# Second attention of a transformer block: longest query tiles first, fill spread by share, fewer product pieces in the last group

## The chip, the cores and the metric

The kernel runs on one NeuronCore of a Trainium2 chip. Its engines work in parallel from queues of their own: TensorE (PE) multiplies matrices into PSUM, with its weight loads shown separately (PEld); VectorE (DVE), ScalarE (ACT) and GpSimd (POOL) work elementwise and reduce; SyncE (SP) starts DMA transfers. They wait for one another through semaphores. The metric is the device time of one execution in microseconds (us), as a median over runs; a profile of one more execution shows where its time goes.

## The reference

A block of four steps over x of 1024 tokens and 512 channels, each `x = x + step(layernorm(x))`: a first attention of 32 heads, an expert layer, a second attention, and the expert layer again. The change touches the second attention alone. It has 32 query heads of width 128 in 8 groups; the 4 heads of a group share keys and values:

```
q = (x @ Wq.T).reshape(b, s, H, HD).transpose(0, 2, 1, 3)
k, v = likewise with Wk, Wv and HKV = 8 heads
q, k = rmsnorm(q) * q_norm_w, rmsnorm(k) * k_norm_w
scores = einsum('bkgqd,bksd->bkgqs', qg, k) / sqrt(HD)
bias = where(rel > 0, NEG_INF, slopes * rel)
attn = softmax(scores + bias, axis=-1)
out = einsum('bkgqs,bksd->bkgqd', attn, v) ... @ Wo.T
```

It is causal: query tile i (128 tokens, i = 0 to 7) sees the first (i + 1) x 128 keys, so tile 7 has eight times the columns of tile 0. All arithmetic is float32.

## The kernel before, in words

The second attention (`attention_b`) loops over groups g, heads hh and query tiles i. For one tile, `softmax(g, hh, i)` makes the scores on TensorE in pieces of up to 512 keys (L778; two PSUM buffers), adds the bias on VectorE (L780), takes the row maximum (L784, scaled at L785), exponentiates on ScalarE with the row sum beside it (L787), takes the reciprocal on VectorE (L789) and normalises on GpSimd (L790). The result p is transposed in 32 x 32 blocks on VectorE by `columns`: the first five key tiles into one buffer PT (L805), which each head overwrites, the last three into TT (L811), which has a place for each head of a group.

`product(g, hh, i0, i1)` multiplies the transposed weights of query tiles i0 to i1, and of the first five key tiles, with the values. It uses matmuls of 32 rows, four of them side by side (L822, tile `o`; one PSUM buffer of four banks), in the order of the key tiles; ScalarE copies the result to oT (L847). `product_rest(g, heads)` does the same with the last three key tiles, for one or more heads at once (L822, tile `or`), and VectorE adds it to oT (L863). In the program one such float32 matmul shows as two instructions.

Between tiles TensorE gets other work, the *fill*: for the next group the projections of keys and values (L687, 8 units of four matmuls) and of queries (L732, 32 units of one matmul, evicted at L741 on ScalarE and L742 on VectorE once in four; sums of squares at L758 and L762), and for the group before the output projection (L628, 32 units, its addition to x on VectorE at L633 once in four units). Their PSUM tiles come from a pool of two buffers. After each tile the loop takes units from the fill until a count `due` is reached: before, `units * n // 32` after n of a group's 32 tiles, with units = 74 (42 in group 0). The last group has no next one; its own counts are in the code: the rest of group 6's output projection in heads 0 and 1, nothing until the 20th tile, and then its own output projection of heads 0 and 1 (two units and one addition for each token tile) and of head 2. Its weights are loaded when head 2 begins. The output projection of head 3 runs in the expert layer that follows.

`finish` of a tile is called two tiles later (LAG = 2): it transposes p, and at the end of a head calls `product`, at the end of a group the rest of all four heads. The last group is different: each head is multiplied in two halves (tiles 0 to 3, then 4 to 7), followed by its own rest. When the program is built, the order of the instructions on each engine may be altered where the dependencies permit.

Of the kernel before, what the change touches and what calls it, by code (L numbers as in the profile page):

```python
# [18 lines left out]
NT = T // P  # L19
# [16 lines left out]
HKV = 8  # L36
GRP = HB // HKV
# [27 lines left out]
class Block:  # L65
# [546 lines left out]
    def attention_b(self, ctx, wo_pool, WqT, WkT, WvT, WoT, qw, kw, xnT, missing, ffn_weights):  # L612
# [9 lines left out]
        oTs = {}  # L622

        def project_o(g, wo, heads, ps_m, tag):
            for t in range(NT):
                ps = ps_m.tile([P, C], F32, tag=tag, name=f"wo{g}_{heads[0]}_{t}")
                for h in heads:
                    nc.tensor.matmul(  # L628
                        ps, lhsT=oTs[g, h][:, t * P : (t + 1) * P], rhs=wo[:, h, :], start=(h == heads[0]), stop=(h == heads[-1])
                    )  # L630
                    if h < heads[-1]:
                        yield
                nc.vector.tensor_add(self.x[t], self.x[t], ps)  # L633
                yield

        with ExitStack() as ctx:
# [23 lines left out]
            def load_qkv(g):  # L660
                wkv = wp.tile([P, self.FFN_SMALL], F32, tag="wkv", name=f"wkv{g}")
                wkv = wkv[:, : KC * 2 * DB].rearrange("p (k n d) -> p k n d", k=KC, n=2)
                for n, src in enumerate((WkT, WvT)):
                    nc.sync.dma_start(wkv[:, :, n, :], src[:, g * DB : (g + 1) * DB].rearrange("(k p) n -> p k n", p=P))
                wq = wp.tile([P, KC, GRP * DB], F32, tag="wq", name=f"wq{g}")
                nc.sync.dma_start(wq, WqT[:, g * GRP * DB : (g + 1) * GRP * DB].rearrange("(k p) n -> p k n", p=P))
                return wq, wkv

            def load_o(g):
                wo = wo_pool.tile([P, GRP, C], F32, tag="wo", name=f"wo{g}")  # L670
                nc.sync.dma_start(wo, WoT[g * GRP * DB : (g + 1) * GRP * DB, :].rearrange("(h p) n -> p h n", p=P))
                return wo
# [130 lines left out]
            def columns(hh, p, i):  # L803
                m = min(JS, i + 1)
                nc.vector.transpose(  # L805
                    PT[:, i : i + (NT - 1) * (m - 1) + 1 : NT - 1, :], p[:, : m * P].rearrange("p (j k) -> p j k", k=P)
                )
                m = i + 1 - JS
                if m > 0:
                    at = i - JS  # L810
                    nc.vector.transpose(  # L811
                        TT[:, hh, at : at + (JT - 1) * (m - 1) + 1 : JT - 1, :],
                        p[:, JS * P : (JS + m) * P].rearrange("p (j k) -> p j k", k=P),
                    )

            def by_groups(g, o, cols, js, moving):

                for j in js:
                    for b in range(NB):
                        for a in range(NB):  # L820
                            rows = slice(a * B, (a + 1) * B)
                            nc.tensor.matmul(  # L822
                                cols(o[:, a], j),
                                lhsT=vs[g][rows, j * NB + b, :],
                                rhs=moving(j, rows, slice(b * B, (b + 1) * B)),
                                start=(j == js[0] and b == 0),
                                stop=(j == js[-1] and b == NB - 1),
                            )

            def queries(t, i0, i1):  # L830

                return t[:, i0 * P : i1 * P].rearrange("p (i a c) -> p a i c", a=NB, c=B)

            def product(g, hh, i0, i1):

                n = i1 - i0
                o = ps_o.tile([P, NB, QC], F32, tag="o", name=f"o{g}_{hh}_{i0}")
                by_groups(
                    g,
                    o,  # L840
                    lambda o, j: o[:, max(j - i0, 0) * B : n * B],
                    range(min(JS, i1)),
                    lambda j, rows, ks: PT[rows, (NT - 1) * j + max(j, i0) : (NT - 1) * j + i1, ks],
                )
                if i0 == 0:
                    oTs[g, hh] = otp.tile([P, T], F32, tag="oT", name=f"oT{g}_{hh}")
                nc.scalar.copy(queries(oTs[g, hh], i0, i1), o[:, :, : n * B].rearrange("p a (i c) -> p a i c", c=B))  # L847

            def product_rest(g, heads):

                n, h0 = len(heads), heads[0]
                o = ps_o.tile([P, NB, QC], F32, tag="o", name=f"or{g}_{h0}")
                by_groups(
                    g,
                    o,
                    lambda o, j: o[:, : n * JT * B].rearrange("p (h q) -> p h q", h=n)[:, :, (j - JS) * B :],
                    range(JS, NT),
                    lambda j, rows, ks: TT[rows, h0 : h0 + n, (JT - 1) * (j - JS) + j - JS : (JT - 1) * (j - JS) + JT, ks],
                )
                for h in heads:  # L860
                    to = queries(oTs[g, h], JS, NT)
                    more = o[:, :, (h - h0) * JT * B : (h - h0 + 1) * JT * B].rearrange("p a (i c) -> p a i c", c=B)
                    nc.vector.tensor_add(to, to, more)  # L863

            def in_turn(*gens):
                for g in gens:
                    yield from g
# [8 lines left out]
            heads = list(range(GRP))  # L876
            rest = []

            def finish(g, hh, i, p):
                while rest:  # L880
                    product_rest(*rest.pop(0))
                columns(hh, p, i)
                if g == HKV - 1:

                    if i == NT // 2 - 1:
                        product(g, hh, 0, NT // 2)
                    elif i == NT - 1:
                        product(g, hh, NT // 2, NT)
                        product_rest(g, [hh])
                elif i == NT - 1:  # L890
                    product(g, hh, 0, NT)
                    if hh == GRP - 1:
                        rest.append((g, heads))

            for g in range(HKV):


                last = g == HKV - 1
                parts = []
                if not last:  # L900
                    wq, wkv = load_qkv(g + 1)
                    parts.append(project_kv(g + 1, wkv))
                    parts.append(project_q(g + 1, wq))
                if g:
                    parts.insert(-1, project_o(g - 1, wo, heads, ps_m, "m"))
                fill = in_turn(*parts)
                units = 74 if g else 42
                done = 0
                for hh in range(GRP):
                    if g and hh == 2:  # L910
                        if last:
                            for _ in fill:
                                pass
                        wo = load_o(g)
                        if last:
                            fill = in_turn(project_o(g, wo, [0, 1], ps_m, "m"), project_o(g, wo, [2], ps_m, "m"))
                    for i in range(NT):
                        p = softmax(g, hh, i)
                        n = hh * NT + i + 1
                        if not last:  # L920
                            due = units * n // (GRP * NT)
                        elif hh < 2:
                            due = max(0, (n - 2) * 32 // 14)
                        else:
                            due = 32 + max(0, 2 * (n - 19)) if n < 27 else 48 + (n - 27)
                        while done < due:
                            next(fill, None)
                            done += 1
                        pending.append((g, hh, i, p))
                        if len(pending) > LAG:  # L930
                            finish(*pending.pop(0))
                    if last and hh == GRP - 1:
                        for item in pending:
                            next(fill, None)
                            finish(*item)
                for _ in fill:
                    pass
                if g == HKV - 2:

                    self.load_ffn(wp, nc.sync, ("wkv", "wq"), *ffn_weights)  # L940
# [156 lines left out]
```

## Time and profile before

| | us |
|---|---|
| runs: median (lowest to highest of 3) | 1710.32 (1709.41 to 1710.95) |
| the profiled execution's own time | 1710.8 |
| its span, first to last instruction | 1709.0 |
| TensorE matmul busy | 1663.4 (97%) |
| VectorE busy | 1110.7 (65%) |
| ScalarE busy | 540.0 (32%) |
| GpSimd busy | 348.8 (20%) |
| second attention, from its first scores | 569 to 1649 |
| expert layer after it | 1649 to 1709 |

How to read the views: a *window* row gives the busy time of each engine within a stretch, and how many instructions it had (x); PEclk is the granted clock of TensorE, 1.00 being full speed. A *group* row gives line, engine, operation, tiles (out<-in), shapes and count, then busy time, the mean of one in ns, and the idle time before such instructions with what ended it. A *wait* row names who waited for whom: us in total, how often, and the longest. A *timeline* row gives start, duration and count of instructions of one kind in sequence; the end of a matmul is modelled and lies some tenths of a microsecond behind the start of the next row, so stretches are measured from start to start.

### The profile page before, as it was taken

How to read it: one execution, taken by the hardware profiler on the slowest of the kernel's cores; microseconds unless marked ns; L12 is line 12 of the kernel's file. 1: busy time of each engine (PE TensorE's matmuls, PEld its weight loads, DVE VectorE, ACT ScalarE, POOL GpSimd, SP SyncE). 2: the span in 40 equal slices, each digit the busy share in tenths (PEclk: the TensorE clock that was granted, in tenths of full speed). 3: DMA queues.
4: the chain of work that ended last, by engine and by line, in shares of the span. 5: the costliest groups of instructions: out<-in, count | busy, mean ns of one | idle time of the engine just before them, and what ended most of it. 6: DMA issues, size and time to landing. Idle time of an engine off the chain costs nothing.

```text
span 1709.0 us, 32010 instructions
## 1 busy us (share of the span) xinstructions
PE 1663.4 (97%) x13040; PEld 940.1 (55%) x13040; DVE 1110.7 (65%) x2872; ACT 540.0 (32%) x1201; POOL 348.8 (20%) x512
## 2 busy tenths in 40 slices
PE   5999999999998999999999999999999999999988
PEld 2544334333555566655665756655665566566654
DVE  3456666663462688677667676677667766777772
ACT  1315555556211333233223223223223322322220
POOL 3000000000311323113212222222311321222140
PEclk9999999999999999999999999999999999999998
DMA  5000000000003210200200110020020021000001
GB/s 191 1 1 2 1 2 1 2 1 1 1 1 112 71 29 26 62 26 26 61 28 1 55 41 19 29 59 26 26 63 26 25 59 37 1 26 26 2 1 49
DMA packets 60356, 51.92 MB, mean 30 GB/s; under 512 B 5489, under 2 KB 46961, under 8 KB 60209
## 3 DMA queue, kind: packets, MB, share of 16 engines
q1 hardware_dynamic: 57840, 43.83, 8.8%
q10 hardware_dynamic: 1584, 3.15, 0.5%
q0 software_dynamic: 784, 2.90, 0.5%
q8 instruction: 102, 1.67, 0.4%
q14 instruction: 46, 0.37, 0.1%
HBM read 30.98 MB, written 2.10 MB: 19 GB/s over the span
## 4 chain that ended last, share of the span: by engine, by line
PE 86%; DVE 10%; ACT 1%; POOL 1%; DMA 1%; issue 0%; SPq 0%; DVEq 0%; ACTq 0%; POOLq 0%
PE o L822 13%; PE pq L732 12%; PE s L778 12%; PE wo L628 9%; PE kv L687 7%; PE sT L347 7%; PE oT L378 4%; PE s L295 3%; PE pm_f L588 3%; PE or L822 3%; DVE p L780 3%; DVE nm L784 2%; DVE pT L805 2%; PE pj_q L166 2%; PE pj_v L166 2%; PE pm_ao L981 2%
## 5 line engine op out<-in xcount | busy, mean ns | idle before, releaser
L790 POOL TENSOR_SCALAR p<-p,rs 128x128 f32<-128x128 f32 (+7 forms) x256 | 190.2, 745 | 751.3 <-DVE rs L789 686.4
L787 ACT ACTIVATE p<-p,nm 128x128 f32<-128x128 f32 (+7 forms) x256 | 198.1, 774 | 453.5 <-DVE nm L785 443.2
L780 DVE SCALAR_TENSOR_TENSOR p<-s,rq,rel 128x512 f32<-128x512 f32 (+3 forms) x384 | 227.6, 607 | 119.5 <-PE s L778 118.9
L778 PE MATMUL s<-kT,qT 128*128 128x512 f32 (+3 forms) x768 | 294.8, 492 | 1.9 <-DVE p L780 1.5
L732 PE MATMUL pq<-xnTb,wq 128*128 128x512 f32 x512 | 246.2, 599 | 0.0
L628 PE MATMUL wo<-wo,oT 128*128 128x512 f32 x512 | 242.0, 594 | 3.4 <-DVE x L633 1.9
L778 PEld LDWEIGHTS s<-kT,qT 128*128 128x128 f32 x768 | 141.2, 190 | 165.9 <-issue 126.4
L822 PEld LDWEIGHTS o<-pT,va 32*128 32x128 f32 x5632 | 215.7, 185 | 28.3 <-DVE rs L789 11.8
L822 PE MATMUL o<-pT,va 32*128 32x128 f32 (+7 forms) x5632 | 224.7, 313 | 0.7
L805 DVE STREAM_TRANSPOSE pT<-p 128x640 f32<-128x640 f32 (+4 forms) x256 | 172.2, 674 | 72.8 <-PE o L822 54.5
L363 ACT ACTIVATE p<-sT 128x512 f32<-128x512 f32 (+1 forms) x320 | 157.5, 557 | 124.9 <-PE s L295 65.9
L784 DVE TENSOR_REDUCE nm<-p 128x1 f32<-128x128 f32 (+7 forms) x256 | 188.6, 737 | 3.6
L295 PE MATMUL s<-kT,qT 32*128 32x512 f32 (+3 forms) x768 | 178.3, 522 | 1.4 <-ACT p L363 1.4
L347 PE MATMUL sT<-qTm,kT 32*128 32x512 f32 (+3 forms) x768 | 152.5, 519 | 0.0
L628 PEld LDWEIGHTS wo<-wo,oT 128*128 128x128 f32 x512 | 93.8, 190 | 87.0 <-issue 72.0
L732 PEld LDWEIGHTS pq<-xnTb,wq 128*128 128x128 f32 x512 | 92.3, 190 | 87.9 <-issue 80.2
L687 PE MATMUL kv<-wkv,xnTb 128*128 128x256 f32 x512 | 118.4, 385 | 9.0 <-DVE nm L785 4.0
L687 PEld LDWEIGHTS kv<-wkv,xnTb 128*128 128x128 f32 x512 | 96.9, 192 | 31.5 <-DVE nm L785 6.9
L312 DVE TENSOR_REDUCE part<-s 128x1 f32<-128x512 f32 x128 | 80.8, 685 | 38.8 <-PE s L295 34.3
L347 PEld LDWEIGHTS sT<-qTm,kT 32*128 32x128 f32 x768 | 59.1, 183 | 66.2 <-issue 22.3
L403 POOL TENSOR_TENSOR o<-os,rsa 128x64 f32<-128x64 f32 x64 | 16.7, 292 | 369.0 <-DVE rsa L401 364.6
L847 ACT COPY oT<-o 128x1024 f32<-128x1024 f32 (+1 forms) x36 | 33.0, 917 | 181.6 <-PE o L822 176.4
(154 smaller groups left out, 1690.8 us busy)
## 6 DMA issues: line engine op xcount, KB each, us to landing
va<-v SPq DMA_DIRECT2D x256, 64.0 KB, 2.0
wq<-in_b_WqT_dram SPq DMA_DIRECT2D x8, 1024.0 KB, 5.3
wo<-in_b_WoT_dram SPq DMA_DIRECT2D x8, 1024.0 KB, 5.3
x<-in_x_dram SPq DMA_DIRECT2D x8, 256.0 KB, 7.9
wkv<-in_b_WkT_dram SPq DMA_DIRECT2D x8, 256.0 KB, 3.1
wkv<-in_b_WvT_dram SPq DMA_DIRECT2D x8, 256.0 KB, 3.4
out_dram<-x SPq DMA_DIRECT2D x8, 256.0 KB, 2.0
wq<-in_a_wqT_dram ACTq DMA_DIRECT2D x1, 1024.0 KB, 6.2
```

The source lines that it names most:

```text
L295: nc.tensor.matmul(made[j][:, at:end], lhsT=qT[rows_of(j), c, i * P : (i + 1) * P], rhs=kT[rows_of(j), c, kc * QC : kc * QC + end - at], s ...
L347: nc.tensor.matmul(made[j][:, at:end], lhsT=kT[rows_of(j), c, b * P : (b + 1) * P], rhs=qTm[c, qc][rows_of(j), QC - (end - at) :], start=n ...
L628: nc.tensor.matmul(ps, lhsT=oTs[g, h][:, t * P : (t + 1) * P], rhs=wo[:, h, :], start=(h == heads[0]), stop=(h == heads[-1]))
L687: nc.tensor.matmul(ps.rearrange("p a b -> p (a b)"), lhsT=xnT[:, kc, i * P : (i + 1) * P], rhs=wkv[:, kc].rearrange("p a b -> p (a b)"), s ...
L732: nc.tensor.matmul(ps, lhsT=wq[:, kc, hh * DB : (hh + 1) * DB], rhs=xnT[:, kc, cols], start=(kc == 0), stop=(kc == KC - 1))
L778: nc.tensor.matmul(s, lhsT=qT[:, i * P : (i + 1) * P], rhs=kT[:, lo:hi], start=True, stop=True)
L780: nc.vector.scalar_tensor_tensor(p[:, lo:hi], s, rq[:, i : i + 1], rel[:, at + lo : at + hi], ALU.mult, ALU.add)
L784: nc.vector.tensor_reduce(nm, p[:, :w], AX.X, ALU.max, negate=True)
L787: nc.scalar.activation(p[:, :w], p[:, :w], AF.Exp, bias=nm, scale=slope, accum_out=ss)
L790: nc.gpsimd.tensor_scalar(p[:, :w], p[:, :w], rs, 1.0, ALU.mult, ALU.mult)
L805: nc.vector.transpose(PT[:, i : i + (NT - 1) * (m - 1) + 1 : NT - 1, :], p[:, : m * P].rearrange("p (j k) -> p j k", k=P))
L822: nc.tensor.matmul(cols(o[:, a], j), lhsT=vs[g][rows, j * NB + b, :], rhs=moving(j, rows, slice(b * B, (b + 1) * B)), start=(j == js[0] an ...
```

## The change

Three things. (1) In all groups, and in the last group for heads 0 to 2, the query tiles of a head run from 7 down to 0; the last head of the last group keeps 0 to 7. A head's product is made when tile 0 is finished. (2) The fill in groups 0 to 6 is due by `SHARE`, a weight for each tile, in place of an equal count: tile 7 and 6 get 42 each of a head's 370, tile 5 gets 70, down to 24 for tile 0. The counts of the last group stay. (3) In the last group heads 0 to 2 are each multiplied in one product of all eight tiles; heads 0 and 1 share one rest, made after head 1's product, and head 2 has one of its own. Head 3 keeps its two halves and its rest.

```diff
@@ product
-                if i0 == 0:
+                if (g, hh) not in oTs:
                     oTs[g, hh] = otp.tile([P, T], F32, tag="oT", name=f"oT{g}_{hh}")
@@ attention_b
+            down = list(reversed(range(NT)))
+
+            SHARE = [24, 34, 42, 54, 62, 70, 42, 42]
+
             def finish(g, hh, i, p):
                 while rest:
                     product_rest(*rest.pop(0))
                 columns(hh, p, i)
-                if g == HKV - 1:
+                last = g == HKV - 1
+                if last and hh == GRP - 1:
 
                     if i == NT // 2 - 1:
                         product(g, hh, 0, NT // 2)
                     elif i == NT - 1:
                         product(g, hh, NT // 2, NT)
                         product_rest(g, [hh])
-                elif i == NT - 1:
+                elif i == 0:
                     product(g, hh, 0, NT)
-                    if hh == GRP - 1:
+                    if last and hh:
+                        product_rest(g, heads[:2] if hh == 1 else [hh])
+                    elif not last and hh == GRP - 1:
                         rest.append((g, heads))
...
-                done = 0
+                done = share = 0
...
-                    for i in range(NT):
+                    for at, i in enumerate(range(NT) if last and hh == GRP - 1 else down):
                         p = softmax(g, hh, i)
-                        n = hh * NT + i + 1
+                        n = hh * NT + at + 1
                         if not last:
-                            due = units * n // (GRP * NT)
+                            share += SHARE[i]
+                            due = units * share // (GRP * sum(SHARE))
```

## The prediction

> **What bounds the kernel now.** The page's first line says that TensorE (PE) is the bound, and VectorE (DVE) the next engine. That is an average, so I cut the second attention (569 to 1649 us) at the first products of its groups, and the last group by head:
>
> ```profile
> PE 1663.4 (97%) x13040; PEld 940.1 (55%) x13040; DVE 1110.7 (65%) x2872; ACT 540.0 (32%) x1201; POOL 348.8 (20%) x512
> ```
>
> ```profile
> core 0: us, PE busy (x) PEld busy (x) DVE busy (x) ACT busy (x) POOL busy (x), PEclk, DMA share, GB/s
> 569.00:676.40 107.40, 107.37 (x796) 68.83 (x798) 91.32 (x238) 40.72 (x103) 37.12 (x48) 1.00 0.16 45
> 676.40:814.60 138.20, 137.18 (x1070) 84.08 (x1070) 96.90 (x236) 40.46 (x98) 35.56 (x47) 1.00 0.13 35
> 1576.00:1607.50 31.50, 31.50 (x437) 20.31 (x436) 24.44 (x57) 8.60 (x20) 6.40 (x9) 1.00 0.02 8
> 1607.50:1649.00 41.50, 38.01 (x687) 25.76 (x687) 31.41 (x66) 7.49 (x15) 10.28 (x13) 1.00 0.01 2
> ```
>
> Group 0, one middle group, and heads 2 and 3 of the last group: PE is full in all but the last, DVE is at 85% in group 0, 70% in a middle group, 76 to 78% at the end. So a better order of the same work can gain only what PE idles. The waits of PE, over the whole span:
>
> ```profile
> PE kv L687 <- DVE nm L785: 4.0, 5, 0.8
> ...
> PE wo L628 <- DVE x L633: 1.9, 2, 1.3
> PE s L778 <- DVE p L780: 1.5, 3, 0.7
> PE wo L628 <- DVE nm L785: 1.4, 2, 0.8
> ```
>
> Five waits of 0.8 us stand one at each start of groups 2 to 6 (a sixth, on wo, at the last group's); the others, some 4 us, all lie in the last group, and all but 0.56 of those in its last head, which keeps its ascending order. Idle PE is thus no source of much gain; less work for PE is.
>
> **What is removed.** In the last group heads 0 to 2 now make one product instead of two halves, and heads 0 and 1 share one rest. PE's rows, a whole product (head 1 of group 2), the rest of four heads, then the second half, the single rest and the next head's first half:
>
> ```profile
> 886.14 6.80 PE L822 MATMUL o<-pT,va 32*128 32x256 f32 x160
> 892.88 1.12 PE L732 MATMUL pq<-xnTb,wq 128*128 128x512 f32 x2
> ```
>
> ```profile
> 1514.83 5.48 PE L822 MATMUL or<-tT,va 32*128 32x384 f32 x96
> 1520.24 1.12 PE L628 MATMUL wo<-wo,oT 128*128 128x512 f32 x2
> ...
> 1576.00 4.75 PE L822 MATMUL o<-pT,va 32*128 32x128 f32 x160
> 1580.68 1.12 PE L628 MATMUL wo<-wo,oT 128*128 128x512 f32 x2
> 1581.73 2.88 PE L822 MATMUL or<-tT,va 32*128 32x96 f32 x96
> 1584.54 1.12 PE L628 MATMUL wo<-wo,oT 128*128 128x512 f32 x2
> ...
> 1590.55 3.77 PE L822 MATMUL o<-pT,va 32*128 32x128 f32 x128
> 1594.25 1.77 PE L778 MATMUL s<-kT,qT 128*128 128x512 f32 x4
> ```
>
> From start to the next row's start: whole 6.74, second half 4.68, first half 3.70, single rest 2.81, rest of four heads 5.41. A block of 32 narrow instructions costs 4.68/5 = 0.94 with 128 columns, and 2.81/3 = 0.94 with 96, 64 and 32: below 128 columns width is free, so cutting work into narrow pieces is what costs. Per head 4.68 + 3.70 - 6.74 = 1.64 is saved, times three 4.9. The rest of two heads has blocks of 192, 128 and 64 columns: the wide blocks of the four-head rest, 5.41 - 0.94 = 4.47 for 640 columns, put 192 at 1.34, the sum at 1.34 + 2 x 0.94 = 3.22; against 2 x 2.81 it saves 2.4. Four entries into a run of such matmuls are gone; each makes the 512-column matmul before it last 0.52 instead of 0.43, 0.4 in all. **Sum: 7.7 us of PE time.** ScalarE copies one 1.01 us output instead of two of 0.58: hidden, it is busy a quarter of the time there. The shared rest has to wait for head 1's copy (the output has one buffer, about 1.2 us with the hop); tile 5's scores (1.29 us) can run between. DVE's additions of rests, 4 x 0.55, stay.
>
> **What is moved: tiles longest first.** Matmuls, vector work and DMAs are the same ones. SyncE's loads and its copies of v keep their place in the fill; GpSimd, 26% busy in a middle group, takes tile 7's 1.12 us normalisation after tile 0's 0.37 and not before it. The instruction order on each engine isn't the source's: the rows show scores of a later tile ahead of a product, and fill ahead of its due, so a late wait is often covered. What must be weighed is the lead of each product: from the scores of the last tile, DVE must get through to that tile's transposition while PE has other work. DVE's per-tile costs come from the rows by shape, for instance:
>
> ```profile
> L780 DVE SCALAR_TENSOR_TENSOR p<-s,rq,rel 128x512 f32<-128x512 f32 x192 | 140.7, 742 | 50.2 <-PE s L778 49.7
> ...
> L784 DVE TENSOR_REDUCE nm<-p 128x1 f32<-128x1024 f32 x32 | 37.9, 1185 | 0.0
> ```
>
> Softmax of tile 7: 2 x 0.742 + 1.185 + 0.136 + 0.155 = 2.96; tile 6 2.71, tile 1 1.17, tile 0 0.88. Transpositions: tile 7 1.39, 6 1.27, 5 1.15 or so, 2 0.58, 1 0.44, 0 0.31. Consecutive rows overlap by some 0.06, so I take 7% off a sum.
> Before, in source order, from tile 7's scores: 2.96 + 1.15 + 0.88 + 1.27 + 1.17 + 1.39 = 8.8, and 7 fill units bring 1.75 evictions of 0.7: 10.0, less 7% 9.3 us of DVE, against PE's 7 x 0.86 + 0.65 of scores = 6.7. After, from tile 0's: 0.88 + 0.58 + 2.96 + 0.44 + 2.71 + 0.31 = 7.9, plus 5.4 units' evictions 0.95: 8.8, less 7% 8.2, against 5.4 x 0.86 + 1.72 + 1.5 = 7.9. The lead is short by 2.6 before, and still PE does not wait; after it is short by 0.3. Groups 1 to 6: **0**. The cover is PE's fill; with none, each product would wait those 5 us.
> Against it: tile 7's transposition writes what all of the previous product reads, where tile 0's writes only its first key block. DVE has then less to do during a product (6.74); tile 6's and 5's softmax, 5.2 us, fill most of it. In group 0, with 10.5 units a head, DVE works 91.32/4 = 22.8 us a head and idles (107.4 - 91.32)/4 = 4.0. Bounds: 0 (those 4.0 did no harm) and, with 1.5 us more idle in each of four products, +6. I take **+1**, nearer the row.
> Group starts: the 0.8 is the wait of kv for a PSUM slot whose reader stands behind tile 7's 1.18 us maximum; now tile 7 of the next group can stand there. Bounds -5 and +5, **0**.
>
> **The last group's heads 1 and 2.** Here fill is due by the old counts: 14 units in head 1, none at head 2's first three tiles (the load of its output weights starts there too: 5.3 us on the page, hidden under a 6.74 us product). Between the products of heads 1 and 2 PE has 6.74 + 3.22 + 5.2 of scores + 14 x 0.86 = 27.2 us. DVE has softmax of tiles 5 to 0 and of head 3's first two 11.9, transpositions 6.7, seven additions to x 4.8, rests 1.1: 24.5, less 7% 22.8, and 5.3 more if tiles 7 and 6 are not done earlier: 28.1, plus waits for exp of 1 to 2. So DVE becomes level with PE there. Bounds 0 and +4; **+1.5**. Head 1's wait of 0.56 goes. The last head's waits, some 3.5, stay.
> [...] The row: after PE's 3.11 us wait at 1667.33 the window 1669 to 1676 has PEclk 0.71, and two 512-column matmuls take 1.91 instead of 1.02. [...] By the row's 6.8 us at half speed, a wait that reaches 3 us at head 1's product, where no fill stands by, would cost another 3.4, and the sum would be near -1.5. I take waits of under 2 us, which in the rows (1.33 at 1637.28) leave the clock at 1.00.
>
> **Sum.** -7.7 + 1 + 1.5 - 0.6 = -5.8. Against the profiled execution (1710.8 around a span of 1709.0) 1705.0; its run is 0.5 above the median 1710.32, so against that 1704.5.
>
> **Rivals.**
> *Even (within 0.2%, 3.4 us, about what runs of this kernel can tell from no change):* DVE becomes the bound of group 0 and of the last group: +5 there and +2 in heads 1 and 2 give the 7.7 back: 1709. For: DVE at 85% in group 0, and less for it to do under a product. Against: PE has no wait there now with a shorter lead.
> *Slower:* the product's wait. DVE takes tiles 7 and 6 of the next head before tile 0's transposition, in all 31 whole products. Break-even is 7.7/31 = 0.25 us a product; at 0.5 it is 15.5 - 7.7 = +7.8: 1718. For: the 0.3 above, and leads set at build time. Against: fill pulled ahead covers 2.6 today.
> *The full gain:* no give-back, the group starts' waits gone: -7.7 - 0.6 - 4 : 1698. For: long maxima no longer end a group; against: one starts the next.
>
> **Numbers.** Main case 0.49 (1700 to 1706.9 by itself), full gain 0.06, together 0.55 for faster; even 0.21; slower 0.24. Below 1700 I leave 0.06, above 1718 0.12: range 1700 to 1718.
>
> **What would show it.** L822 counts 5632 + 1056 falling by 480; whole products of about 6.7 us in the last group and one 3.2 us rest; group windows still 138 to 139 us; group 0 within 107 to 109. Wrong if PE gets waits on pT ahead of o (slower), if group 0 grows by 5 us (even), or if clock dips appear inside the attention.

## The result, and where the time went

The changed kernel takes 1705.27 us (median of 9 runs, 1704.12 to 1707.02), the kernel before in the same runs 1710.86 (1708.82 to 1713.35). The ratio is 0.9969, with a 95% interval of 0.9958 to 0.9979: 5.6 us faster, where 5.8 was forecast. The sum behind it was less good than that looks.

TensorE has less to do, 1657.1 against 1663.4 us busy, and 480 instructions fewer. The line is the page's first, of the changed kernel:

```profile
PE 1657.1 (97%) x12560; PEld 934.2 (55%) x12560; DVE 1113.7 (65%) x2872; ACT 541.7 (32%) x1198; POOL 349.7 (21%) x512
```

Cut by stage, again from product to product (group 0 from its first scores, two middle groups, then the last group from the product of head 1 to that of head 2, and its last stretch):

```profile
core 0: us, PE busy (x) PEld busy (x) DVE busy (x) ACT busy (x) POOL busy (x), PEclk, DMA share, GB/s
...
569.00:680.30 111.30, 109.69 (x793) 68.91 (x791) 93.53 (x240) 41.67 (x102) 37.89 (x48) 1.00 0.16 44
680.30:818.90 138.60, 137.84 (x1068) 84.41 (x1067) 97.37 (x234) 40.95 (x95) 35.22 (x46) 1.00 0.13 35
818.90:957.20 138.30, 137.54 (x1065) 84.46 (x1064) 97.72 (x234) 40.15 (x95) 35.24 (x46) 1.00 0.12 35
...
1567.40:1596.30 28.90, 27.79 (x303) 18.11 (x302) 22.85 (x59) 8.45 (x19) 6.35 (x9) 1.00 0.03 11
1596.30:1645.00 48.70, 44.07 (x691) 29.66 (x690) 32.98 (x73) 8.52 (x17) 11.53 (x14) 0.96 0.01 2
```

Measured from one group's rest to the next, groups 2 to 5 take 138.4 us each, 138.8 before. Group 0's row isn't to be compared with 107.4 as it stands: its last product is now behind tiles 7 and 6 of the next head, 2.6 us more of scores. Five short waits, 1.5 us together, are new in it. The last row has what is new besides: TensorE idles 4.6 us in it, and PEclk is below 1. TensorE's waits in the whole span, of the changed kernel:

```profile
PE s L778 <- DVE p L780: 3.1, 9, 1.1
PE wo L628 <- DVE x L633: 3.1, 1, 3.1
PE kv L687 <- DVE qT L742: 3.0, 6, 0.6
...
PE tp_f L98 <- DVE oT L863: 1.2, 1, 1.2
...
PE wo L628 <- DVE rs L789: 0.9, 1, 0.9
```

At five group starts the wait on kv fell from 0.81 to 0.57, and in each of groups 1 to 6 one of 0.19 on scores came. One of 3.1 us stands in the last head.

For a count that doesn't depend on where a product stands I take the stretch from the first scores of this attention to the first transposition of the last expert layer (tp_f), and sum TensorE's start-to-start intervals by line, its waits over 0.15 us apart. Differences to the kernel before, in us:

| | stretch | product `o` | rest `or` | waits | scores, fill and others |
|---|---|---|---|---|---|
| before | 1079.2 | 222.1 | 49.1 | 8.9 | |
| changed | -2.75 | -4.1 | -2.4 | +3.45 | +0.3 |

Of the profiled pair's other 2.5 us, 2.2 lie in the last expert layer and 0.3 ahead of the attention. About 1.2 of the 2.2 come with the change. Where no slow clock falls into that layer, it takes 57.7 us from the mark when the last group ascends (two profiles below) and 56.5 when its first three heads descend (two others). So the wait of 1.2 on tp_f, which the table counts, is won back behind the mark, and 2.2 of the 3.45 remain. The other 1.0 is the clock: a spell at half speed costs the layer 2.6 us before (it lasts 6.8) and 1.7 after (3.4). Such spells differ from execution to execution (the nine runs of the changed kernel have mean clocks of 0.995 to 0.997), and are part of why single runs of a kernel lie 1 to 5 us apart; the differences of medians are what is judged.

### The profile page after: what moved, and what is told of

The parts are those of the page before. It is cut to its first block, busy times and chain, and to the rows that moved or that the text cites. A ratio compares the mean times of both kernels' runs of the same rounds, so it can differ in the third digit from the quotient of the medians.

```text
span 1703.8 us, 30960 instructions
## 1 busy us (share of the span) xinstructions
PE 1657.1 (97%) x12560; PEld 934.2 (55%) x12560; DVE 1113.7 (65%) x2872; ACT 541.7 (32%) x1198; POOL 349.7 (21%) x512
## 4 chain that ended last, share of the span: by engine, by line
PE 88%; DVE 6%; ACT 2%; POOL 2%; DMA 1%; issue 1%; SPq 0%; DVEq 0%; ACTq 0%; POOLq 0%
PE s L778 13%; PE o L822 12%; PE wo L628 12%; PE pq L732 11%; PE sT L347 7%; PE kv L687 6%; PE oT L378 4%; PE s L295 3%; PE pm_f L588 3%; PE or L822 2%; PE pj_q L166 2%; PE pj_v L166 2%; PE pm_ao L992 2%; PE pj_k L166 2%; DVE pT L805 1%; DVE p L780 1%
## 5 line engine op out<-in xcount | busy, mean ns | idle before, releaser
L787 ACT ACTIVATE p<-p,nm 128x1024 f32<-128x1024 f32 (+7 forms) x256 | 198.2, 774 | 447.9 <-DVE nm L785 425.6
L790 POOL TENSOR_SCALAR p<-p,rs 128x1024 f32<-128x1024 f32 (+7 forms) x256 | 191.0, 747 | 687.8 <-DVE rs L789 656.4
L732 PE MATMUL pq<-xnTb,wq 128*128 128x512 f32 x512 | 240.9, 597 | 0.0
L822 PEld LDWEIGHTS o<-pT,va 32*128 32x128 f32 x5248 | 210.8, 185 | 26.0 <-issue 18.4
L822 PE MATMUL o<-pT,va 32*128 32x256 f32 (+5 forms) x5248 | 220.3, 321 | 0.1
L784 DVE TENSOR_REDUCE nm<-p 128x1 f32<-128x1024 f32 (+7 forms) x256 | 187.5, 735 | 2.3
L378 PE MATMUL oT<-p,v_p 128*32 128x256 f32 (+3 forms) x1024 | 86.8, 417 | 0.0
```

The lines of the kernel that those rows point to most:

```text
L732: nc.tensor.matmul(ps, lhsT=wq[:, kc, hh * DB : (hh + 1) * DB], rhs=xnT[:, kc, cols], start=(kc == 0), stop=(kc == KC - 1))
L784: nc.vector.tensor_reduce(nm, p[:, :w], AX.X, ALU.max, negate=True)
L787: nc.scalar.activation(p[:, :w], p[:, :w], AF.Exp, bias=nm, scale=slope, accum_out=ss)
L790: nc.gpsimd.tensor_scalar(p[:, :w], p[:, :w], rs, 1.0, ALU.mult, ALU.mult)
L822: nc.tensor.matmul(cols(o[:, a], j), lhsT=vs[g][rows, j * NB + b, :], rhs=moving(j, rows, slice(b * B, (b + 1) * B)), start=(j == js[0] an ...
```

## The experiments

The runs stand in three batches, each with its own runs of the kernel before: the first four below (before: 1710.66, 33 runs), shares in the last group and one rest for three heads (1710.25, 16 runs), and the other four (1710.60, 16 runs). The diffs are against the changed kernel, unless another is named. Beside its time each run has a mean granted clock of TensorE, given to 0.001; by arithmetic, 3.4 us at half speed in a run of 1705 lower it by 0.001 and cost up to 1.7 us.

**The pieces alone.** Does the work taken out explain the gain, or the order?

```diff
-                elif i == 0:
+                elif i == NT - 1:
...
-                    for at, i in enumerate(range(NT) if last and hh == GRP - 1 else down):
+                    for at, i in enumerate(range(NT)):
...
-                            due = units * share // (GRP * sum(SHARE))
+                            due = units * n // (GRP * NT)
```

> Only the third part of the change: heads 0 to 2 of the last group in one product each, heads 0 and 1 with one rest; all tiles ascending and fill by equal count as before. Theory WORK (the gain is the TensorE work taken out of the last group, 6.5 to 7 us; the order gives nothing): 1704 to 1706 us, some 6 below the kernel before, groups 0 to 6 as before (138.8 a middle group). Rival ORDER (the gain is the order of the tiles and the spread of the fill): within 1.5 us of the kernel before, since VectorE's waits swallow the work taken out.

Measured: 1701.31 us, ratio 0.9942 (0.9929 to 0.9954): 9.4 us faster than before, and 4 us faster than the whole change. By the traces the stretch is 8.2 us shorter than before: products -5.1, rests -2.4, scores and output projection -1.1, waits +0.4. Two windows of it, a middle group and the last group from the product of group 6's last head on, and its waits:

```profile
core 0: us, PE busy (x) PEld busy (x) DVE busy (x) ACT busy (x) POOL busy (x), PEclk, DMA share, GB/s
...
813.80:952.60 138.80, 137.77 (x1068) 84.41 (x1067) 96.71 (x234) 39.83 (x94) 35.10 (x46) 1.00 0.12 35
1505.50:1640.00 134.50, 129.94 (x1513) 82.94 (x1513) 101.98 (x227) 31.81 (x67) 28.17 (x37) 1.00 0.03 9
```

```profile
PE kv L687 <- DVE nm L785: 4.1, 5, 0.8
...
PE wo L628 <- DVE x L633: 1.9, 2, 1.3
PE s L778 <- DVE p L780: 1.9, 2, 1.0
```

The middle group is as before, the waits nearly so; only the last group is shorter (142.7 before, between the same marks). WORK stands, though the time lies 2.7 below its range, and it was the whole of the gain and more. Part of the 9.4 is clock: all five runs have a mean of 0.998, those of the kernel before 0.995 to 0.998. Its three runs at 0.998 have a median of 1709.14, 7.8 above this one; these are few runs, but the figure is that of the work removed.

**The order alone.** The last group as in the kernel before, groups 0 to 6 as changed.

```diff
-                if last and hh == GRP - 1:
+                if last:
...
-                    for at, i in enumerate(range(NT) if last and hh == GRP - 1 else down):
+                    for at, i in enumerate(range(NT) if last else down):
```

> Only the first two parts, and only in groups 0 to 6: tiles descending, fill by SHARE; the last group ascending, in halves, with its own rests as before. Theory WORK: 0 to +2 us against the kernel before (1711 to 1713): group 0 some 1.5 us longer by TensorE waits, the waits at the starts of groups 0.57 instead of 0.81 (-1.4 in all), the 0.19 waits of middle groups +0.9. Rival ORDER: -4 to -6 us, about 1705.

Measured: 1710.44, ratio 1.0005 (0.9996 to 1.0013), no difference; in the traces the stretch is 1.2 us longer, its waits 1.8. ORDER has fallen; WORK's account holds, its range is missed by 0.6.

**Two single rests.** Is the shared rest worth its work, or is it in VectorE's shadow?

```diff
-                    if last and hh:
-                        product_rest(g, heads[:2] if hh == 1 else [hh])
+                    if last:
+                        product_rest(g, [hh])
```

> The changed kernel with one rest for each of heads 0 and 1 instead of one for both. Theory WORK: the two single rests of 2.81 us come back for one of 3.24, so +2.4 us on the changed kernel (1707.7), 3.2 below the kernel before. Rival LEVEL (VectorE bounds heads 1 and 2 of the last group, so TensorE work there is free): less than +0.8 on the changed kernel, 1705 to 1706.

Measured: 1709.09, ratio 0.9991 (0.9985 to 0.9998), 3.8 us above the changed kernel, 1.4 more than WORK had. By the traces the rests take 2.4 more (49.1 against 46.7), as counted; the output projection takes 1.5 more because the slow clock lasted 6.8 us in this profile. At the same mean clock, 0.997, the five runs of this kernel (median 1707.65) lie 2.4 above the five of the changed one (1705.21). LEVEL has fallen: TensorE's work counts in heads 1 and 2.

**Equal fill with descending tiles.**

```diff
-                            due = units * share // (GRP * sum(SHARE))
+                            due = units * n // (GRP * NT)
```

> The changed kernel with the fill by equal count again instead of by SHARE. Theory FREE ORDER (the build moves fill to where TensorE would wait, so its source position is worth nothing in groups 1 to 6): within 1 us of the changed kernel, 1704.5 to 1706.5, with middle groups at 138.4 and at most group 0 longer by 1 or 2. Rival SHARE (fill must stand beside the long tiles): DVE lags behind TensorE by some 1 us in each of tiles 5 to 2, waits of 0.5 to 1 us a head in 28 heads, +10 us or more, 1716 and up.

Measured: 1717.32, ratio 1.0038 (1.0026 to 1.0051), 12 us above the changed kernel. FREE ORDER was wrong: the descending order needs SHARE. The time is in the rival's range, but the waits aren't in 28 heads, as it had them. Its waits of TensorE:

```profile
PE s L778 <- DVE p L780: 7.2, 9, 1.2
PE st L758 <- ACT qsq L741: 6.7, 7, 1.1
```

They add up to 22.0 us in the stretch against 12.3, nearly all of the difference of 10.1. In each of groups 1 to 6 there are two, 0.76 near the end of the first head and 1.08 at the group's end, where of its fill only the sums of squares are left; a middle group takes 139.6.

**No fill under the long tiles.** The forecast's rival "slower", made real: by the source hardly any fill stands between a head's last scores and its product.

```diff
-            SHARE = [24, 34, 42, 54, 62, 70, 42, 42]
+            SHARE = [0, 34, 42, 54, 62, 70, 0, 0]
```

> The changed kernel with shares of 0 for tiles 0, 7 and 6, so that by the source only 1.5 units of fill stand between the last scores of a head and its product, against 5.4. Theory BOUNDARY (the build moves fill between the heads of a group, so that only the starts of groups can wait): no wait at the products inside a group, the waits at the starts of groups grow by 0.5 to 2 us each, 1708 to 1719. Rival LEAD (each product waits for VectorE where the source gives no cover): waits of 0.4 us and more ahead of nearly all 31 whole products, 1717 and up. Rival FREE (places of fill are worth nothing): within 1 us of the changed kernel.

Measured: 1714.31, ratio 1.0023 (1.0014 to 1.0031), 9 us above the changed kernel. Not one product of groups 1 to 6 has a wait ahead of it, so LEAD is refuted. The built order explains it: VectorE makes tile 0's transposition early, and not behind the softmax of tiles 7 and 6. In the changed kernel, group 2, it stands ahead of tile 7's maximum and 3.9 us before the product:

```profile
854.17 0.30 DVE L805 STREAM_TRANSPOSE pT<-p 128x128 f32<-128x128 f32 x1
...
855.13 1.22 DVE L784 TENSOR_REDUCE nm<-p 128x1 f32<-128x1024 f32 x1
...
858.36 6.80 PE L822 MATMUL o<-pT,va 32*128 32x256 f32 x160
```

Of the 28 products of groups 0 to 6, 23 start 3.9 us or more after that transposition ends; with this fill taken away all 28 still start 0.3 to 0.8 after it. BOUNDARY had the time and no wait at the products, but not the form: the waits at group starts grow from 0.57 to 0.84 only. The 1.4 us a group lie elsewhere: in five groups the rest is cut in two runs (4.2 us more in all), and scores, kv and the sums of squares have wider intervals that aren't waits by the profile's measure. What widens them wasn't settled.

**The last group ascending, the rest of the change kept.** Where do the 4 us lie that the whole change loses to its pieces?

```diff
-                elif i == 0:
+                elif i == (NT - 1 if last else 0):
...
-                    for at, i in enumerate(range(NT) if last and hh == GRP - 1 else down):
+                    for at, i in enumerate(range(NT) if last else down):
```

> The changed kernel, but the last group's heads ascend as before; groups 0 to 6 stay descending with SHARE, and the last group keeps its larger products and shared rest. Theory LAST (the order costs its 4 us in the last group, where the fill counts were not adapted; in groups 0 to 6 it is free, as the run with the order alone showed): about the time of the run with the pieces alone, 1701 to 1702.5, and no wait near 3 us in the last head. Rival SUM (the order costs the same whatever the last group does): as the changed kernel, 1704.5 to 1706.

Measured: 1704.35 with runs from 1700.93 to 1706.21, ratio 0.9959 (0.9947 to 0.9972). The median is only 0.9 below the changed kernel's, and time alone doesn't tell LAST from SUM. The runs follow the clock: two at a mean of 0.999 took 1700.93 and 1701.64, one at 0.996 1704.35, two at 0.994 1705.14 and 1706.21. The profile is of the fastest, so it shows where the order can cost, not how much it costs in a usual run. In it the stretch is 1072.5, 1.45 us above the pieces alone (the price of the order in groups 0 to 6, as in the run of the order alone) and 4.0 below the changed kernel: waits 1.3 (about what is won back behind the mark), output projection 2.05, products 0.8. The changed kernel's rows for these, the products of heads 0 and 1 of the last group, its shared rest, and the last head:

```profile
1539.88 6.80 PE L822 MATMUL o<-pT,va 32*128 32x256 f32 x160
1546.61 1.56 PE L778 MATMUL s<-kT,qT 128*128 128x512 f32 x4
...
1565.07 0.69 PE L822 MATMUL o<-pT,va 32*128 32x256 f32 x2
1565.70 1.77 PE L778 MATMUL s<-kT,qT 128*128 128x512 f32 x4
1567.40 6.79 PE L822 MATMUL o<-pT,va 32*128 32x256 f32 x158
...
1575.61 3.31 PE L822 MATMUL or<-tT,va 32*128 32x192 f32 x96
1578.85 1.35 PE L778 MATMUL s<-kT,qT 128*128 128x512 f32 x4
...
1628.26 1.12 PE L628 MATMUL wo<-wo,oT 128*128 128x512 f32 x2 [3.10 <-DVE x L633]
1630.26 4.51 PE L628 MATMUL wo<-wo,oT 128*128 128x512 f32 x6 [0.87 <-DVE rs L789]
```

The product of head 1 is broken after two instructions by scores of head 2, and entered twice. The rest of two heads takes 3.24. And the last head has one wait of 3.10. VectorE's rows ahead of it, in the changed kernel:

```profile
1623.90 0.84 DVE L805 STREAM_TRANSPOSE pT<-p 128x640 f32<-128x640 f32 x1 [0.93 <-POOL p L790]
1624.67 0.40 DVE L811 STREAM_TRANSPOSE tT<-p 128x256 f32<-128x256 f32 x1
1624.99 1.37 DVE L780 SCALAR_TENSOR_TENSOR p<-s,rq,rel 128x512 f32<-128x512 f32 x2
1626.40 1.22 DVE L784 TENSOR_REDUCE nm<-p 128x1 f32<-128x1024 f32 x1
1627.53 0.68 DVE L633 TENSOR_TENSOR x<-x,wo 128x512 f32<-128x512 f32 x1
```

The addition to x that frees the PSUM tile stands behind tile 6's transpositions and the bias and maximum of tile 7. In the two ascending kernels the last head has four waits of 0.6 to 1.33, 3.5 together. After the 3.10 the clock falls:

```profile
core 0: us, PE busy (x) PEld busy (x) DVE busy (x) ACT busy (x) POOL busy (x), PEclk, DMA share, GB/s
1626.00:1630.40 4.40, 1.27 (x3) 0.47 (x4) 3.59 (x7) 1.24 (x2) 0.12 (x1) 1.00 0.00 0
1630.40:1633.80 3.40, 3.40 (x5) 1.34 (x6) 1.58 (x3) 0.00 (x0) 1.00 (x1) 0.50 0.01 2
```

These 3.4 us at half speed cost 1.7, most of the 2.05. All five profiled kernels with this 3.1 us wait (the changed one, single rests, equal fill, no fill under the long tiles, and shares in the last group) have such a spell within 6 us of the wait's beginning, 3.4 us long in two of them and 6.8 in three; before, the order alone, the pieces alone and this one have none inside the attention. These five are the kernels whose last group descends in heads 0 to 2 and ascends in head 3, so LAST is right about the wait. How much of the 4 us it makes in a usual run is not shown.

**Shares in the last group too.** Are its unadapted counts to blame?

```diff
                         elif hh < 2:
-                            due = max(0, (n - 2) * 32 // 14)
+                            share += SHARE[i]
+                            due = 32 * share // (2 * sum(SHARE))
```

> The changed kernel with SHARE also for the fill of heads 0 and 1 of the last group (group 6's output projection), in place of the equal count of 32 units over 14 tiles. Theory COUNTS (the last group's order costs 4 us because the equal count of its heads 0 and 1 does not fit descending tiles): 1702 to 1703.5, the 1.1 us wait in head 2 gone. Rival TAIL (the cost sits in heads 2 and 3, behind those counts: the 3.1 us wait on the evictions of the last head and the slow clock that follows it): within 1 us of the changed kernel, 1704.3 to 1706.3, with a wait near 3 us still in the last head.

Measured: 1706.71, ratio 0.9979 (0.9970 to 0.9988). COUNTS has fallen: the waits of 1.11 in head 2 and 3.10 in the last head are unchanged. TAIL has the place right, the time is 0.4 beyond its range.

**The last head descending**, in one product and one rest; once in the changed kernel, as this diff shows, and once in the pieces alone.

```diff
-                if last and hh == GRP - 1:
-
-                    if i == NT // 2 - 1:
-                        product(g, hh, 0, NT // 2)
-                    elif i == NT - 1:
-                        product(g, hh, NT // 2, NT)
-                        product_rest(g, [hh])
-                elif i == 0:
+                if i == 0:
...
-                    for at, i in enumerate(range(NT) if last and hh == GRP - 1 else down):
+                    for at, i in enumerate(down):
```

> The changed kernel with the last head descending too, in one product and one rest, its halves gone. Theory TAIL WAITS (the last head's 5.2 us of TensorE waits come from its long tiles standing at the end, where no fill is left): 1.6 us of TensorE work less and 1 to 3 of the waits gone, 1701 to 1703. Rival EXPOSED (a whole product at the very end leaves the last tile's chain, 3 us, and the copy and rest, 1.2, without cover): within 1 us of the changed kernel or above it, 1704.5 to 1708.

> The kernel with the pieces alone (all ascending, equal fill) and its last head descending in one product and one rest. Theory TAIL WAITS: 1.6 us of work and 1 to 2 of the 3.5 us of waits less than with the pieces alone (1701.3): 1698 to 1700. Rival EXPOSED: 1700.5 to 1704.

Measured: 1703.60 (0.9964, 0.9951 to 0.9976) in the changed kernel, 1.7 less than it, which is not clear of noise; 1704.82 (0.9963, 0.9950 to 0.9975) in the pieces alone, 3.5 more. The work falls by 1.6 to 1.9 in both. In the changed kernel the 3.10 becomes 0.82, 1.17 and 0.77, and a rest that waits 1.14 for the copy; in both a wait of 1.81 appears early in the expert layer. TAIL WAITS is missed by 0.6 in the first, EXPOSED by 0.8 upward in the second: descending in the last head trades one tail for another.

**One rest for three heads**, from the pieces alone. The output projection of the later token tiles must then wait for it.

```diff
-                    if last and hh:
-                        product_rest(g, heads[:2] if hh == 1 else [hh])
+                    if last and hh == 2:
+                        product_rest(g, heads[:3])
...
-                            due = 32 + max(0, 2 * (n - 19)) if n < 27 else 48 + (n - 27)
+                            due = 32 + min(10, max(0, 2 * (n - 19))) if n < 27 else 48 + (n - 27)
```

> The kernel with the pieces alone, with one rest for heads 0, 1 and 2 together after head 2's product, and the last group's own output projection held at five token tiles (10 units) until then, as the later ones need the rest. Theory WORK: the rests of 3.24 and 2.81 become one with blocks of 288, 192 and 96 columns, 2.0 + 1.34 + 0.94 = 4.3 us, so -1.8 us on the pieces alone (1701.3): 1699 to 1700.5. Rival HELD FILL (with six units held back head 2 runs out of fill and head 3 gets too much at once): 1701 to 1705.

Measured: 1705.26, ratio 0.9969 (0.9957 to 0.9981), 4 us above the pieces alone. Its rows at head 2's end:

```profile
1589.83 0.91 PE L778 MATMUL s<-kT,qT 128*128 128x384 f32 x2 [1.88 <-DVE p L780]
1591.67 1.99 PE L778 MATMUL s<-kT,qT 128*128 128x512 f32 x4 [0.94 <-DVE p L780]
...
1602.03 4.39 PE L822 MATMUL or<-tT,va 32*128 32x288 f32 x96
...
1608.60 8.19 PE L628 MATMUL wo<-wo,oT 128*128 128x512 f32 x18 [1.12 <-DVE oT L863]
```

The rest takes 4.32 to the next row's start and saves 1.74, as expected (1.8); but without fill TensorE waits 1.88, 0.94 and 1.12. HELD FILL has the cause right and the time 0.3 beyond its range: fill is worth more than the blocks saved.

## Why the prediction was right, and which step was off

*Bound.* Right. TensorE was full, and removing its work is what gained.

*Work removed, -7.7.* Right, and confirmed alone: -7.5 by lines in the pieces alone. The rest of two heads was put at 3.22 and took 3.24; the whole products take 6.73. In the changed kernel one product is entered twice, so only -6.5 remains.

*Order in groups 0 to 6, +1 in all.* Right in size and place: +1.2 and +1.45 in two pairs of traces, unmeasurable in runs; group 0's new waits make 1.5, and in groups 1 to 6 the shorter waits at the starts and the new ones on scores nearly cancel. The reasoning under it was only partly so. The lead of the product (short by 0.3 after, 2.6 before) was counted with all of tile 7's and 6's softmax ahead of tile 0's transposition; in the built order it ends 3.9 us or more before most products. So the lead decided nothing. By the same count equal fill (7 units for a product against 5.4) should have been at least as good, and it cost 12 us: fill runs short at group ends, not at products.

*Last group's heads 1 and 2, +1.5, less 0.6.* A wait of 1.11 in head 2 for the 0.56 in head 1: +0.55. Smaller than taken, and as signed. VectorE did not become level with TensorE: it was busy 22.9 of the 28.9 us between the two products, the lower of the two figures weighed. The sum's 14 units are those of head 2; head 1 has 19 by the counts in the code.

*"The last head's waits, some 3.5, stay."* This is the step that failed. The last head's source order is untouched, but the build orders it anew behind the altered heads: 5.2 us of waits (3.10, 0.87, 1.20) and a spell at half clock, 1.7. As the 1.20 is won back, that is 2.2 us more than the forecast had, in this profile. The forecast weighed a spell behind a wait of 3 us at head 1's product, from the 3.11 and the 6.8 us at half speed in the last expert layer before. No wait near 3 us came there (1.11 is the longest in heads 1 and 2); one came in the last head, and its spell cost 1.7 where 3.4 was weighed. So one of the forecast's own signs of being wrong, a clock dip inside the attention, did appear.

*The close hit is partly luck.* In the profiled pair the stretch gained 2.75, some 4.0 with what is won back, where 5.8 was summed. Some 1.3 more came from a shorter spell in the last expert layer and from ahead of the attention. The medians over runs can't be split by stage.

*Rivals.* No product of a kernel with the change had a wait on pT; the one in any run, 0.29 us, is in the last head of the pieces alone with that head descending. "Even" put its losses in the wrong place. The full gain, 1698, was not reached; the pieces alone, the fastest kernel here, comes nearest, and by other means, as its group starts keep their waits.

## What to carry to other kernels

Where one engine is full and nearly without waits, count the instructions that leave it, and try that edit by itself before joining it to a new order: here 4 of 9 us were gone when the order was added. A block of these narrow matmuls took 0.94 us at 128 columns, and as much on the average of 96, 64 and 32, so narrow pieces saved no time here: merge them while fill still covers what must then wait. An order that is set at build time can shift waits into code whose source isn't touched; the end of a stage, where no fill is left, is where to look first.

## What was not expected of the hardware

The slow clock isn't tied to one wait of 3 us. The last head descending in the changed kernel has no wait over 1.17 in its last 30 us of attention, but two spells of 3.4 us at half speed: PEclk is 0.83 in each of the windows 1620 to 1630 and 1630 to 1640. The forecast took waits of under 2 us as harmless, by one of 1.33 that left the clock at 1.00. And the same waits can come with a spell and without. These are the output projection's matmuls in the last head, with one rest for three heads (first two rows) and with the last group ascending (last two):

```profile
1627.55 1.12 PE L628 MATMUL wo<-wo,oT 128*128 128x512 f32 x2 [0.60 <-DVE nm L785]
1630.01 3.64 PE L628 MATMUL wo<-wo,oT 128*128 128x512 f32 x4 [1.33 <-DVE x L633]
...
1627.54 1.12 PE L628 MATMUL wo<-wo,oT 128*128 128x512 f32 x2 [0.60 <-DVE nm L785]
1630.00 1.96 PE L628 MATMUL wo<-wo,oT 128*128 128x512 f32 x4 [1.33 <-DVE x L633]
```

The waits are the same, 0.60 and 1.33, and begin within 0.01 us of each other. Behind them the same four instructions take 3.64 us in the first profile and 1.96 in the second, whose PEclk is 1.00 from 1620 to 1640. The mean clocks of the two profiled runs are 0.994 and 0.999.

In the profiles of the kernel before and of the changed one, from 40 us on, TensorE has five waits over 1.33 us, and each has a spell at a clock of 0.50 beside it:

| profile | wait, us | ends at | spell begins at | spell lasts, us |
|---|---|---|---|---|
| before | 3.70 | 519.6 | 519.4 | 3.4 |
| before | 3.11 | 1667.3 | 1666.3 | 6.8 |
| changed | 3.45 | 518.5 | 517.7 | 6.8 |
| changed | 3.10 | 1628.3 | 1630.4 | 3.4 |
| changed | 2.63 | 1663.0 | 1664.5 | 3.4 |

Three spells begin while TensorE still waits, two 1.5 and 2.1 us after the wait. The length doesn't follow the wait: 3.70 has 3.4 us, 3.11 has 6.8. The next longest waits of the two profiles, 1.33, 1.20 and 1.11, have no spell within 10 us. So a wait's length alone doesn't tell, over all these profiles, whether a spell comes or whether it lasts 3.4 or 6.8 us. What decides it is not shown. The idle times rest on modelled ends of matmuls.
